# Taking a state-space scan's first half sequence inside an earlier stage, with its sum in SBUF

## The chip, the core and the metric

The kernel runs on one core of a Trainium2 chip. The time is device microseconds of one execution. The core has a matrix engine (PE, with a separate queue for loading weights, PEld), a vector engine (DVE), an activation engine (ACT), a general engine (POOL) and a queue that issues most of the transfers (SP). Each engine works off its own list of instructions in a fixed order; an instruction that has to wait holds up those behind it in the same list. All data are float32.

## The reference

Eight layers follow each other; each is a residual sum and a layer norm over x of shape 4 x 1024 x 128 (batch, sequence, features). The ones that matter here are the last four:

```
# linear attention with 16 heads of 64: running sums over the sequence
S_cos += k_cos v^T ; S_sin += k_sin v^T ; z_cos += k_cos ; z_sin += k_sin
out_t = (q_cos S_cos + q_sin S_sin) / max(q_cos z_cos + q_sin z_sin, 1e-6)

# top-2 mixture of 8 experts, hidden width 256
h = silu(gate) * up ; y = sum over the two chosen experts of weight * (h @ w2)

# state-space layer: 256 channels e, 16 states n
x = rmsnorm(resid) ; skip = x @ skip_w.T ; xs = silu(conv4(x @ in_w.T))
delta = softplus(...) ; B = xs @ wb.T ; C = xs @ wc.T
h[e,n] = exp(delta[e] * A[e,n]) * h[e,n] + delta[e] * xs[e] * B[n]    # over t
y[e]  = sum over n of h[e,n] * C[n]
out = resid + ((y + xs * W_D) * silu(skip)) @ out_w.T

# top-p mixture of 8 experts, hidden width 512, all experts computed
y = sum over e of gate[e] * (relu(x @ W1[e] + b1[e]) @ W2[e] + b2[e])
```

The scan over t of each (e, n) is a first-order recurrence. The two norms between these layers tie a batch's next layer to the end of its last one, but batches are independent of each other.

## The kernel before

x is held in SBUF twice for each batch: xN (tokens on partitions) and xT (features on partitions, 128 x 1024). A tile framework records the program in Python; generators yield between pieces, so that pieces of several layers are interleaved. The framework orders each engine's list itself, by the order in which the pieces were recorded and by its own estimate of when an operand is there; only PE's list inside the linear attention is kept as recorded (manual_schedule in l2_attn).

**Linear attention (l2_attn, line 920).** 128 units: 4 batches x 4 quarters of 256 tokens x 8 pairs of heads. A loop over t records pieces of units t to t + 2: l2_project makes q and k two units ahead (PE pqk, ACT r_q and r_k, and two POOL multiplications qt, L1059), l2_keys and l2_scores one unit ahead (kN on ACT, a on DVE), l2_before and l2_within consume qt and a, and l2_sums adds the running state (st on DVE). PSUM tiles pa, kp and po are single; qt has 3 buffers, a has 2.

**Top-2 experts (l2_dispatch, l2_ffn, l2_combine).** When a batch leaves the linear attention, l2_dispatch routes it on DVE and scatters its rows to DRAM with 16 indirect transfers from POOL (xrows, one with each step). l2_ffn then works through 23 tiles of 128 rows for each batch: rows 8 steps ahead, weights (wx, 384 KB, 4 buffers) 4 ahead, transposed tile 2 ahead, hidden layer, and two steps later the output. A step is one next() on the generator; the attention's loop makes one in each unit. When a unit 8 steps ahead belongs to a batch that has not been scattered, the whole pipeline stands. l2_combine gathers the outputs of a half batch back with 8 indirect transfers from POOL (yg), scales them on ACT and norms; a batch is marked "done" after its second half.

**State-space layer (l3, line 1595).** 8 half sequences (4 batches x 2 halves of 512 tokens). l3_prepare makes dl (delta), ud (delta times xs), xs and the rows of B and C in DRAM; its first call, for the very first half, is recorded inside the attention's loop once batch 0 is done, one piece in each unit, with batch 0 to 2's xT as scratch (l3_early, L1694). l3_scan (L1819) then takes 16 states n for each half. For each it issues two broadcasting transfers from SP (bn, cn: 128 x 512 each), one POOL multiplication db = ud * bn (L1849), two ACT exponentials da into PSUM (L1853), two DVE scans (L1854), one POOL multiplication hc = db * cn (L1865) and the sum over n by PE, a matmul with the identity for each of two channel halves (pys, L127). From batch 1 on, two states are first added by an accumulating transfer from POOL's queue (L1870), which halves those matmuls. l3_sum, l3_gate and l3_finish end a half: skip gate, output projection, norm, router. While half i is scanned, half i + 1 is prepared, half i - 1 is ended, top-2 tiles of later batches go on (one step a state, two in the first half), and three or four steps of the last layer's experts run.

**Last experts (l3_experts, l3_ffn).** For a half that has been ended for more than 3 states, 8 experts: 4 matmuls ph of 512 columns, ACT relu hh, 16 matmuls py, and a DVE accumulation h_acc each.

Of the kernel before, what the change touches and what calls it, by code (L numbers as in the profile page):

```python
# [10 lines left out]
F32 = mybir.dt.float32  # L11
# [47 lines left out]
class Net:  # L59
# [860 lines left out]
    def l2_attn(self, load, dispatch, moe, first):  # L920
# [7 lines left out]
        with ExitStack() as ctx:  # L928
# [25 lines left out]
            side, begin = [], None  # L954
# [9 lines left out]
            for t in range(-2, n + 4):  # L964
# [329 lines left out]
    def l2_dispatch(self, b):  # L1294
# [86 lines left out]
        for c in range(NC):  # L1381
            for k in range(2):
# [15 lines left out]
                yield  # L1398
# [3 lines left out]
    def l2_ffn(self, wp):  # L1402
# [8 lines left out]
        n = len(units)  # L1411
        side = []
        for t in range(-8, n + 4):
            while t + 8 < n and "put" not in units[max(t + 8, 0)]["st"]:
                for g in side[:]:
                    if next(g, self) is self:
                        side.remove(g)
                yield
            if 0 <= t + 8 < n and units[t + 8]["j"] % 4 == 0:
                self.l2_load_rows(units[t + 8], units, t + 8, wp)  # L1420
            if 0 <= t + 4 < n:
                self.l2_weights(units[t + 4], wp)
            if 0 <= t + 2 < n:
                self.l2_load_tile(units[t + 2], units, t + 2, wp)
            if 0 <= t < n:
                self.l2_hidden(units[t], wp)
            if 0 <= t - 2 < n:
                u = units[t - 2]
                self.l2_expert_out(u, units, t - 2, wp)
                if u["j"] == NT2 - 1:  # L1430
                    side.append(self.l2_combine(u["st"], wp))
# [4 lines left out]
        for g in side:  # L1436
            yield from g
# [81 lines left out]
    def l2_combine(self, st, wp):  # L1519
# [18 lines left out]
        for h in range(2):  # L1538
# [21 lines left out]
            yield from self.norm_parts(wp, acc, b, 4 * h, 4, ps=self.bank("ff"), act=True, slow=True, rows=False)  # L1560
        st["done"] = True
# [33 lines left out]
    def l3(self, moe, fp):  # L1595
# [12 lines left out]
        end = iter(())  # L1608
        for i, u in enumerate(halves):
            nxt = iter(())  # L1610
            if i + 1 < len(halves):
                if halves[i + 1]["h"] == 0:
                    while "done" not in self.m2["st"][halves[i + 1]["b"]]:
                        next(moe)
                nxt = self.l3_prepare(halves[i + 1])
# [594 lines left out]
```

## Time and profile before

| what | value |
|---|---|
| median of 3 runs (lowest, highest) | 2288.26 us (2287.27, 2295.73) |
| the profiled execution | 2286.79 us, its span 2285.0 us |
| busy in the span: PE, DVE, ACT, POOL | 87%, 59%, 53%, 45% |
| layers 1 to 4 | 0 to 615 us |
| linear attention, with top-2 experts woven in from 951 us | 615 to 1335 us |
| state-space layer and last experts | 1335 to 2285 us |
| first half's scan (first db to last hc) | 1390 to 1476 us |
| second half's scan | 1476 to 1569 us |
| tail after the last scan: last experts only | 2150 to 2285 us |

A line of the windows view gives, for a stretch of the span, the busy time of each engine with the number of its instructions, then the granted PE clock, the busy share of the transfer engines and GB/s. A line of the groups view gives source line, engine, operation, out<-in, shapes, count, then busy us and mean ns of one, then the idle time of the engine just before these instructions and what ended it. A line of a tile's view gives min/median/max ns of one.

### The profile page before, as it was taken

What the parts mean: (1) busy time and instruction counts of PE and PEld (TensorE: products, weight loads), DVE (VectorE), ACT (ScalarE), POOL (GpSimd) and SP (SyncE); (2) the same over time, 40 slices, a digit from 0 to 9 for tenths busy, and PEclk for the clock granted to TensorE, in tenths of its full rate; (3) what the DMA queues carried; (4) which work ended last, traced back from release to release, by engine and by line L of the source; (5) the groups of instructions that cost most, each with busy time, mean ns of one, the idle gap of its engine ahead of it and who ended that gap; (6) DMA issues with size and microseconds to landing.
All of it is one profiled execution on the core that took longest, in us unless ns stands there. A gap on an engine that the chain in (4) does not pass through costs nothing.

```text
span 2285.0 us, 46402 instructions
## 1 busy us (share of the span) xinstructions
PE 1978.9 (87%) x17806; PEld 1383.3 (61%) x17806; DVE 1349.2 (59%) x3693; ACT 1210.5 (53%) x2623; POOL 1023.4 (45%) x812
## 2 busy tenths in 40 slices
PE   6667979879999999999989876679899999999998
PEld 3455655444477777787767664246565656565666
DVE  6457843433355565565555555696777688776521
ACT  6543443332244444444455456576768786767443
POOL 5100230000023234224233418998889889879400
PEclk9667989979999999999999988799999999999999
DMA  3000110005000010031223147456786677776421
GB/s 107 0 14 24 30 39 1 19 10 174 1 3 2 3 35 15 17 87 49 65 80 85 37 126 221 135 175 200 216 216 178 174 189 192 193 187 167 119 61 51
DMA packets 138559, 211.10 MB, mean 92 GB/s; under 512 B 18598, under 2 KB 75937, under 8 KB 137953
## 3 DMA queue, kind: packets, MB, share of 16 engines
q1 hardware_dynamic: 126192, 173.87, 25.5%
q0 software_dynamic: 12144, 34.26, 7.1%
q8 instruction: 140, 2.29, 0.4%
q14 instruction: 83, 0.67, 0.1%
HBM read 160.29 MB, written 23.16 MB: 80 GB/s over the span
## 4 chain that ended last, share of the span: by engine, by line
PE 43%; DVE 12%; ACT 11%; issue 3%; DMA 2%; POOL 1%; SPq 0%; ACTq 0%; DVEq 0%; POOLq 0%
PE py L127 7%; PE ph L127 7%; PE po L1126 5%; PE pqk L127 5%; PE pa_m L127 5%; DVE db L1854 4%; PE pys L127 3%; PE kp_mo L127 3%; PE pv L127 2%; PE pr L1196 2%; ACT hh L1980 1%; ACT da L1853 1%; PE pt L131 1%; PE kp_mo L131 1%; ACT xN L174 1%
## 5 line engine op out<-in xcount | busy, mean ns | idle before, releaser
L1059 POOL TENSOR_TENSOR qt<-r_q,sb_c_turn 128x256 f32<-128x256 f32 (+1 forms) x256 | 164.0, 660 | 447.9 <-ACT r_q L1051 442.2
L1865 POOL TENSOR_TENSOR hc<-db,cn 128x1024 f32<-128x1024 f32 x128 | 314.7, 2493 | 57.1 <-PE pys L127 25.6
L127 PEld LDWEIGHTS py<-wh,hh 128*128 128x128 f32 x2048 | 249.8, 192 | 79.9 <-issue 44.8
L1849 POOL TENSOR_TENSOR db<-ud,bn 128x1024 f32<-128x1024 f32 x112 | 286.3, 2633 | 12.4 <-issue 9.9
L127 PE MATMUL ph<-xT,wh 128*128 128x512 f32 x512 | 256.3, 618 | 21.2 <-DVE h_acc L1996 5.8
L127 PE MATMUL py<-wh,hh 128*128 128x128 f32 x2048 | 258.2, 276 | 12.7 <-ACT hh L1980 6.6
L1980 ACT ACTIVATE hh<-ph,sb_cols 128x512 f32<-128x512 f32 x256 | 170.6, 680 | 131.1 <-PE ph L127 104.5
L1117 DVE TENSOR_TENSOR a<-pa_m,sb_c_near 128x256 f32<-128x256 f32 x256 | 96.6, 419 | 203.4 <-PE pa_m L127 203.4
L1074 ACT ACTIVATE kN<-kp_mo,sb_c_trig 128x128 f32<-128x128 f32 x448 | 129.8, 371 | 132.0 <-PE kp_mo L131 122.2
L1853 ACT ACTIVATE da<-dl,aneg 128x512 f32<-128x512 f32 x224 | 153.6, 689 | 74.4 <-DVE db L1854 73.3
L127 PE MATMUL pys<-hc,sb_c_ident 128*128 128x512 f32 x324 | 158.5, 619 | 22.7 <-POOL hc L1865 19.4
L1854 DVE TENSOR_TENSOR_SCAN db<-da,carry,db 128x512 f32<-128x512 f32 x128 | 156.9, 1265 | 11.7 <-ACT da L1853 8.8
L1854 DVE TENSOR_TENSOR_SCAN db<-da,db 128x512 f32<-128x512 f32 x128 | 149.3, 1205 | 10.4 <-POOL db L1849 6.0
L127 PEld LDWEIGHTS ph<-xT,wh 128*128 128x128 f32 x512 | 89.6, 196 | 104.7 <-issue 53.5
L1996 DVE SCALAR_TENSOR_TENSOR h_acc<-py,gt,h_acc 128x128 f32<-128x128 f32 x256 | 71.9, 342 | 125.8 <-PE py L127 125.8
L127 PE MATMUL pqk<-xT,wE 128*128 128x256 f32 x512 | 136.7, 390 | 8.3 <-ACT coT L1193 4.2
L127 PEld LDWEIGHTS pys<-hc,sb_c_ident 128*128 128x128 f32 x324 | 60.5, 199 | 86.7 <-issue 58.7
L729 POOL DMA_INDIRECT orows<-o,ix x20 | 18.9, 944 | 186.0 <-DVE o L727 160.4
L127 PEld LDWEIGHTS pqk<-xT,wE 128*128 128x128 f32 x512 | 88.5, 193 | 21.9 <-DVE cv L1036 8.1
L131 PE MATMUL pt<-sb_c_ident,xN 128*128 128x128 f32 x224 | 54.2, 345 | 51.0 <-ACT xN L174 31.8
L1193 ACT COPY coT<-pt 128x512 f32<-128x512 f32 x64 | 37.5, 586 | 114.9 <-PE pt L131 114.9
L127 PE MATMUL po<-ht,wD 128*128 128x512 f32 x192 | 93.7, 595 | 0.0
(456 smaller groups left out, 4344.1 us busy)
## 6 DMA issues: line engine op xcount, KB each, us to landing
wx<-in_wF SPq DMA_DIRECT2D x92, 384.0 KB, 3.4
bn<-rows SPq DMA_DIRECT2D x128, 256.0 KB, 5.0
cn<-rows SPq DMA_DIRECT2D x128, 256.0 KB, 4.2
wh<-in_wH SPq DMA_DIRECT2D x64, 512.0 KB, 3.8
hc<-hc POOLq DMA_DIRECT2D x47, 512.0 KB, 6.6
xrows<-zero SPq DMA_DIRECT2D x4, 1472.0 KB, 12.3
xg<-xrows SPq DMA_DIRECT2D x20, 256.0 KB, 3.0
yrows<-ys SPq DMA_DIRECT2D x20, 256.0 KB, 3.3
```

Of the source, the lines that this page charges most:

```text
L127: return self.nc.tensor.matmul(out=out, lhsT=lhsT, rhs=rhs, start=start, stop=stop)
L131: self.nc.tensor.transpose(out, in_, self.ident[0:n, 0:n])
L1059: nc.gpsimd.tensor_mul(u["qt"][:, m, a:], u["q"][:, a:], c2["turn"][:, m, o + a : o + 2 * P])
L1074: self.nc.scalar.activation(u["kN"][:, c, m, :], pk[:, c, :], AF.Copy, scale=trig[:, k, m : m + 1])
L1117: nc.vector.tensor_mul(u["a"][:, i, :, :], pa[i], self.c2["near"][:, None, :].to_broadcast([P, 2, P]),)
L1126: self.nc.tensor.matmul(out=u["po"][self.HALF[j], i, c, :], lhsT=lhsT, rhs=rhs, start=key not in u["begun"], stop=True, skip_group_check=True,
L1849: nc.gpsimd.tensor_mul(db, ud, bc[0])
L1853: nc.scalar.activation(da, dl[:, ec, :], AF.Exp, scale=aneg[:, j : j + 1])
L1854: nc.vector.tensor_tensor_scan(db[:, ec, :], da, db[:, ec, :], carry[:, ec, n : n + 1] if h else 0.0, ALU.mult, ALU.add,)
L1865: nc.gpsimd.tensor_mul(hc, db, bc[1])
L1980: nc.scalar.activation(ht, ph, AF.Relu, bias=self.col("h_b1", i=e * NK + k))
L1996: nc.vector.scalar_tensor_tensor(acc[:, c, :], py[:, c, :], gt[:, c, e : e + 1], acc[:, c, :], ALU.mult, ALU.add,)
```

## The change

Four parts.

1. The early preparation starts when batch 0's first half has been combined ("half"), not when both have. It is followed by a new generator l3_first, which takes the first half's 16 states inside the attention's loop. The recorded steps are spread evenly over the units that are left (left, 10 + 2 * 16 steps). Its working set differs from l3_scan's: bn, cn and db have 2 buffers; da goes to SBUF, one buffer for each channel half (the first is the weight tile wgru of the first layer); db is multiplied on DVE for odd n and on POOL for even n; and the sum over n is kept in SBUF in batch 0's xT (acc): n = 0 writes it, and each further state is added by an accumulating transfer from POOL's queue, each of which has to wait for the one before. The matmuls pys of this half are gone.
2. l2_ffn goes by the age of its tiles: each tile in flight passes stages at ages 0 (rows), 1 (weights), 3 (transposed tile), 5 (hidden), 7 (output), so tiles in flight go on when the next batch has not been scattered. The combining generators get two steps for each.
3. Batch 0's 16 scatters are recorded two to a step (no yield after the first of a pair for b = 0).
4. l3 no longer scans the first half: a prologue ends it while the second half is prepared, with one top-2 step and two scatter steps for each piece; then 7 halves are scanned, with two top-2 steps a state for the first two of them (halves 1 and 2). l3_gate moves from the scan into the end for halves where the scan hasn't made it.

The pool of the dispatch's tiles (md) is opened earlier. Cut to its core:

```diff
-                    if "done" in self.m2["st"][0]:
-
+                    if "half" in self.m2["st"][0]:
                         if begin is None:
-                            begin = self.l3_prepare(self.l3_early(first))
-                        next(begin, None)
+                            scan = ctx.enter_context(tc.tile_pool(name="scan", bufs=2))
+                            u = self.l3_early(first, scan)
+                            begin = chain(self.l3_prepare(u), self.l3_first(u, scan))
+                        for k in range(1 if "dl" not in u else max(1, -(-left // max(1, n - t)))):
+                            next(begin, None)
+                            left -= 1
...
-                yield
+                if k or b:
+                    yield
...
+        side, live, k = [], [], 0
+        stages = (
+            (0, lambda i: units[i]["j"] % 4 == 0 and self.l2_load_rows(units[i], units, i, wp)),
+            (1, lambda i: self.l2_weights(units[i], wp)),
+            (3, lambda i: self.l2_load_tile(units[i], units, i, wp)),
+            (5, lambda i: self.l2_hidden(units[i], wp)),
+            (7, lambda i: self.l2_expert_out(units[i], units, i, wp)),
+        )
+        while k < len(units) or live or side:
+            if k < len(units) and "put" in units[k]["st"]:
+                live.append([k, 0])
+                k += 1
+            for at, f in stages:
+                for i, age in live:
+                    if age == at:
+                        f(i)
+            for v in live:
+                v[1] += 1
+            if live and live[0][1] > 7:
+                i = live.pop(0)[0]
+                if units[i]["j"] == NT2 - 1:
+                    side.append(self.l2_combine(units[i]["st"], wp))
...
+            st["half"] = h
...
+        def ending(u):
+            for ec in range(2):
+                if len(u.get("gate", ())) == ec:
+                    self.l3_gate(u, ec)
+            yield from self.l3_sum(u)
+            yield from self.l3_finish(u)
+        end = ending(halves[0])
+        for f in following(0):
+            next(end, None)
+            next(moe, None)
+            for k in range(2):
+                next(self.m2["rest"], None)
+        for i, u in enumerate(halves[1:], 1):
+            nxt = following(i)
...
+                for k in range(2 if i < 3 else 1):
+                    next(moe, None)
...
+            if name == "ud":
+                return scan.tile(shape, F32, name=name, bufs=1)
...
+        u["acc"] = two(self.xT[0])
+        u["carry"] = pool.tile([P, 2, NST], F32, name="carry0")
+        u["wide"] = wide
...
+    def l3_first(self, u, pool):
+        nc, aneg = self.nc, self.c3["aneg"]
+        dl, ud, rows, acc, carry = (u[k] for k in ("dl", "ud", "rows", "acc", "carry"))
+        for n in range(NST):
+            bc = []
+            for i, nm in enumerate(("bn", "cn")):
+                t = pool.tile([P, 1, 512], F32, name=nm)
+                r = i * NST + n
+                nc.sync.dma_start(
+                    out=t[:, 0, :], in_=rows[r : r + 1, :].to_broadcast([P, 512])
+                )
+                bc.append(t.to_broadcast([P, 2, 512]))
+            db = pool.tile([P, 2, 512], F32, name="db")
+            (nc.vector if n % 2 else nc.gpsimd).tensor_mul(db, ud, bc[0])
+            yield
+            for ec in range(2):
+                j = ec * NST + n
+                da = pool.tile([P, 512], F32, name="da", bufs=1) if ec else u["wide"]
+                nc.scalar.activation(da, dl[:, ec, :], AF.Exp, scale=aneg[:, j : j + 1])
+                nc.vector.tensor_tensor_scan(
+                    db[:, ec, :], da, db[:, ec, :], 0.0, ALU.mult, ALU.add
+                )
+            nc.scalar.copy(carry[:, :, n : n + 1], db[:, :, 511:512])
+            hc = db if n else acc
+            nc.gpsimd.tensor_mul(hc, db, bc[1])
+            if n:
+                nc.gpsimd.dma_start(out=acc, in_=db, accum_op=ALU.add)
+            yield
+        u.update(py=[acc[:, ec, :] for ec in range(2)], sums=[])
```

More of the change, by code (lines that the diff above doesn't have):

```diff
@@ L953, in l2_attn @@
             n = len(units)
-            side, begin = [], None
+            side, begin, left = [], None, 10 + 2 * NST
             def early(moe):
@@ L1410, in l2_ffn @@
         ]
[L1411 to L1431, printed above, removed]
+        side, live, k = [], [], 0
[20 more added lines that the diff above has]
+                    side.append(self.l2_combine(units[i]["st"], wp))
             for g in side * 2:
@@ L1435, in l2_ffn @@
             yield
-        for g in side:
-            yield from g
     def l2_load_rows(self, u, units, i, wp):
@@ L1607, in l3, with following @@
         work = self.l3_experts(fp)
[L1608 to L1615, printed above, removed]
+        def following(i):
+            if i + 1 == len(halves):
+                return iter(())
+            if halves[i + 1]["h"] == 0:
+                while "done" not in self.m2["st"][halves[i + 1]["b"]]:
+                    next(moe)
+            return self.l3_prepare(halves[i + 1])
+        def ending(u):
[12 more added lines that the diff above has]
+            nxt = following(i)
             u["final"] = i + 1 == len(halves)
@@ L1622, in l3 @@
                     next(nxt, None)
-                for k in range(1):
-                    next(self.m2["rest"], None)
-                next(moe, None)
-                if i == 0:
-                    for k in range(1):
-                        next(moe, None)
+                next(self.m2["rest"], None)
+                for k in range(2 if i < 3 else 1):
+                    next(moe, None)
                 for k in range(4 if n % 8 == 7 else 3):
@@ L1634, in l3 @@
                 pass
-            end = chain(self.l3_sum(u), self.l3_finish(u))
+            end = ending(u)
         for f in end:
@@ L1692, in l3_at, with l3_early @@
         return pool.tile(shape, F32, name=name, tag=tag)
-    def l3_early(self, pool):
-        half = lambda b, i: self.xT[b][:, i * 512 : (i + 1) * 512]
+    def l3_early(self, pool, scan):
+        half = lambda i: self.xT[0][:, i * 512 : (i + 1) * 512]
+        two = lambda x: x.rearrange("p (e t) -> p e t", e=2)
+        wide = self.wgru.rearrange("p a b -> p (a b)")
         k = [0]
@@ L1702, in at @@
                 return pool.tile(shape, F32, name=name)
-            if name in ("dl", "ud"):
-                return self.xT[1 if name == "dl" else 2].rearrange("p (e t) -> p e t", e=2)
+            if name == "dl":
+                return two(self.xT[1])
+            if name == "ud":
+                return scan.tile(shape, F32, name=name, bufs=1)
             if name == "sq3":
-                return half(2, 0).rearrange("p (k d) -> p k d", d=D)
+                return half(0).rearrange("p (k d) -> p k d", d=D)
@@ L1707, in at @@
             if name == "db1":
-                return half(2, 1)[0:ND]
+                return wide[0:ND]
             if name == "xc":
                 k[0] += 1
-                return half(0, k[0] % 2)
-            return half(0, name == "sp_w")[:, None, :]
+                return half(k[0] % 2)
+            return half(name == "sp_w")[:, None, :]
         u = dict(b=0, h=0, at=at, ff=self.bank("pj"))
+        u["acc"] = two(self.xT[0])
+        u["carry"] = pool.tile([P, 2, NST], F32, name="carry0")
@@ L2177, in program @@
             w2 = ExitStack()
+            md = w2.enter_context(tc.tile_pool(name="moed", bufs=1, side="right"))
             n.l2_attn_load(w2.enter_context(tc.tile_pool(name="w2", bufs=1, side="right")))
@@ L2187, in program @@
         with w2:
-            md = w2.enter_context(tc.tile_pool(name="moed", bufs=1, side="right"))
             n.l2_attn(load, n.l2_dispatch, moe, first)
```

## The prediction

> **What bounds the kernel now.** I read the page first (shares and the 40 slices), then the windows by stage, the groups, the tile's view of gru_z and the transfers.
>
> ```profile
> PE 1978.9 (87%) x17806; PEld 1383.3 (61%) x17806; DVE 1349.2 (59%) x3693; ACT 1210.5 (53%) x2623; POOL 1023.4 (45%) x812
> PE   6667979879999999999989876679899999999998
> DVE  6457843433355565565555555696777688776521
> POOL 5100230000023234224233418998889889879400
> PEclk9667989979999999999999988799999999999999
> ```
>
> PE is the busiest engine, but not in every stage. The windows show it: us of the stretch, then busy time of PE, PEld, DVE, ACT, POOL.
>
> ```profile
> 960.00:1170.00 210.00, 198.72 (x3357) 166.66 (x3356) 126.59 (x470) 100.61 (x301) 64.78 (x99) 0.99 0.24 66
> 1170.00:1215.00 45.00, 34.27 (x497) 27.70 (x497) 22.31 (x92) 31.18 (x91) 20.81 (x27) 0.89 0.29 80
> 1335.00:1566.00 231.00, 163.88 (x741) 108.17 (x740) 161.16 (x326) 139.20 (x304) 186.97 (x104) 0.87 0.60 180
> 1566.00:2150.00 584.00, 533.16 (x2642) 346.31 (x2640) 437.92 (x844) 426.78 (x767) 510.32 (x263) 0.99 0.70 188
> 2150.00:2285.00 135.00, 120.87 (x678) 86.64 (x676) 33.05 (x118) 53.14 (x84) 0.00 (x0) 0.97 0.20 58
> ```
>
> In the linear attention (960 to 1170) PE is busy 95% of the time and POOL 31%. After it (1335 to 1566) PE falls to 71% while POOL, with the first two halves' multiplications, is at 81%: this is the hole that the change aims at. Later PE (91%) and POOL (87%) are both near full. The prices of the moved work:
>
> ```profile
> L1865 POOL TENSOR_TENSOR hc<-db,cn 128x1024 f32<-128x1024 f32 x128 | 314.7, 2493 | 57.1 <-PE pys L127 25.6
> L1849 POOL TENSOR_TENSOR db<-xT,bn 128x1024 f32<-128x1024 f32 x16 | 37.6, 2372 | 0.1
> L1854 DVE TENSOR_TENSOR_SCAN db<-da,db 128x512 f32<-128x512 f32 x128 | 149.3, 1205 | 10.4 <-POOL db L1849 6.0
> L235 DVE TENSOR_TENSOR_SCAN gru_h<-gru_a,gru_z 128x512 f32<-128x512 f32 x8 | 12.9, 1612 | 3.6 <-POOL gru_z L233 3.6
> ```
>
> Two lines of tiles' views (ns: min/median/max, then first to last start in us; the second within 1060 to 1160):
>
> ```profile
> L233 POOL TENSOR_TENSOR gru_z<-gru_z,gru_g x16: 1252/1749/2159, 12.0 to 57.7; 128x512 f32<-128x512 f32 x16
> L1051 ACT ACTIVATE r_q<-pqk,sb_cols x18: 473/482/511, 1064.1 to 1159.2; 128x256 f32<-128x256 f32 x18
> ```
>
> One line of the transfers (KB, us to landing) and one of PE's waits in 1160 to 1215 (us, times, longest):
>
> ```profile
> hc<-hc POOLq DMA_DIRECT2D x47, 512.0 KB, 6.6
> ...
> PE kp_mo L131 <- ACT ys L1510: 8.0, 4, 2.9
> ```
>
> To see: the scan takes 1.205 us with da in PSUM, but 1.61 us in the first layer, where both operands lie in SBUF and POOL multiplies beside it; POOL's 128x512 multiplication there took between 1.25 and 2.16 us, median 1.75. An accumulating transfer of 512 KB lands 6.6 us after its issue (median; shortest 4.5).
>
> **The change part by part.** The sum is made against the profiled execution, 2286.8 us; the median of the runs, 2288.3, is 1.5 us above it. 0.5% (11.4 us) is about what a measurement of this kernel can tell from no change.
>
> *Where the moved scan lands.* By the recorded order, combine of batch 0 now begins in unit 82 (before 102), half 0 is there in unit 88, the preparation ends in unit 99 (before 125), and the states are recorded one in two units, to 129. The lists of the engines say otherwise: in the built order POOL's 16 states stand between the qt of units 102 and 115, and DVE's scans between the a of units 101 and 114: 13 units, because the framework pulls ahead what it thinks ready. A unit there takes 5.88 us (34 r_q in 960 to 1160), so 76 us of attention carry the whole scan.
>
> *POOL in these 13 units.* 8 db and 16 hc: 24 x 2.36 = 57; 13 pairs of qt (0.728 each): 19; 15 issues of accumulating transfers (1.04): 16; 4 scatters: 4. Sum 96 us in 76. To this comes: (a) the scans' da is now in SBUF, as in the first layer. By gru_z's median over its minimum, 0.5 us for a multiplication of 512 columns, counted 0.5 to 1.0 for 1024: 12 to 24, taken 15. (b) Each accumulating transfer waits on POOL for the one before. Between neighbours in the list lie only 1.4 to 4.8 us of other POOL work in 9 of 14 cases; with 4.5 to 6.6 us to landing the waits add up to 12 to 31 us, taken 21. db has two buffers, so the product two states on waits for the same landing; I count that in the upper end. (c) hc waits for its scans: 57.1 us of idle over 128 = 0.45 each, 16 x 0.45 = 7. Together 139 us.
>
> *DVE in the same units.* Attention and tiles 3.15 us a unit (80.3 us in 1000 to 1150) = 41; batch 2's routing, some 45 small operations of 0.2, 10; 32 scans x 1.62 = 52; 8 products of 1024 columns, 2 x 0.684 (the nearest row, yg + yg, 128x512) = 11; the end of the preparation 3: 117 us. It is inside POOL's 139, but both lists run against PE's in a fixed order, so DVE is no way out. ACT has 32 exponentials x 0.69 + 16 copies x 0.19 = 25 us more on 48% busy, about 62 in 139: hidden. SP issues 32 broadcasts more; the transfer engines are at 24% here, so they are covered, but cn of state n + 2 stands in SP's list until hc of n is done, with a wx behind it; wx has 4 buffers, which cover a delay of about two units.
>
> *What it does to PE.* po of a unit needs its qt, which is made two units ahead; 8 us of lead are used up first. Loss in the attention: 139 - 76 - 8 = **+55**. Lower end: POOL's own work alone, 96 - 76 - 8 = +12. Upper end: 43 (gru_z's maximum, 0.9 for 512 columns, twice that for 24) and 31 for the waits, 7 for (c): 177 - 84 = +93. I take the middle because (a) and (b) are each taken at their typical row.
>
> A rule of the Trainium skill speaks against the change here: SBUF — State Buffer, Who interferes with whom, says that a DVE instruction with two SBUF inputs and a GpSimd one that reads SBUF exclude each other for the whole instruction. The gru rows agree in kind (1.61 against 1.205). Taken at full, 39 + 11 us of such DVE work would add to POOL's 96, 146 - 84 = +62, and the time would be 2311 instead of mine.
>
> *The second combine.* combine of batch 1 moves from after the attention into its last units (122 on). The same work cost before: 6 units in 1160 to 1215 instead of 9.4, 20 us, of which 8.0 are PE behind ACT's ys, which stands behind the scaling of gathered rows. Half of it falls past the last unit: **+10** (0 to +20). Batch 0's combine moves from 102 to 82 and costs the same there: 0.
>
> *Tiles by age.* 46 tiles instead of 43 are done in the attention: 3 x 1.9 us (8 rows 1.13, 4 rows 0.61, transpose 0.15) go from one side to the other: 0. Batch 0's scatters end in unit 52 instead of 60, each pair 2.5 us on a POOL that was idle 70%: 0.
>
> *After the attention.* Before: 55 us to the first db, 86 for half 0, 93 for half 1: 1335 to 1569, 234 us. After: a prologue to the first db of half 1, then its scan. The prologue must prepare half 1 (from 1346 to 1445, 99 us, beside a scan; 11 units, 65 us, in the attention), end half 0, run 14 tiles and pass the 8 gathers and 16 scatters (24 x 1.28 = 31 us of POOL): taken 80, between 60 and 99. The scan 93, plus 5 for gathers that move into it: 178 us, so -56. That holds the 27.5 us of PE that go (32 pys of 4 rows at 1.72 for two). Then 6 halves as before: POOL 87%, PE 91%, neither relieved in them. The tail doesn't shrink: in the built order some 317 last-expert matmuls stand behind the last half's pys against 296, because the experts, though begun sooner, go behind the denser tiles: 21 x 0.35 (7.0 us for an expert's 20) = +8 rounded. Together **-48** (-68 to -29).
>
> **Sum:** 2286.8 + 55 + 10 - 48 = 2303.8, **2304 us**, 0.7% slower.
>
> **The rivals.**
> *The attention covers the scan* (faster, the other side). For it: POOL idle 69% and DVE 40% between 960 and 1170. Against it: the 13 units. At the lower end: 2286.8 + 12 + 10 - 48 = 2261. It decides from the point where the 13 units take under 111 us (loss under 27 instead of 55).
> *Even.* A loss of 27 to 49: at 38, 2287.
> *The accumulating transfers set the pace.* Two buffers of db in a ring of product (2.4), scans (2.4), hc (2.4), issue (1.0) and landing (6.6), stretched by other POOL work: at a loss of 85, 2286.8 + 85 + 10 - 48 = 2334. For it: the 6.6 us. Against it: that median was taken at 70% busy transfer engines, here 24%.
> *The scan isn't taken inside the attention*: excluded by the built order, where the last hc stands 14 units before the end.
>
> **How the numbers follow.** Forecast (loss 49 to 75, 2298 to 2324) 0.38; deep 0.20; even 0.16; covered 0.26. Slower by over 0.5%: forecast and deep, 0.58; within: 0.16; faster: 0.26. The range 2255 to 2342 leaves about 0.1 on either side: the covered case with the prologue at 70 instead of 80, and the deep case up to a loss of 93.
>
> **What will show it.** In the profile after: units 102 to 115 at 9 to 11 us each instead of 5.9, with POOL near 90% busy and PE near 60% there; the new hc at over 2.6 us mean and its scans at 1.5 us or more; the end of the attention 55 to 70 us later than 1335; the first db of half 1 some 80 us after it; no pys for half 0; a tail of 135 to 145 us. Wrong if the units in the stretch stay under 8 us (then faster), or if the later halves fall under 90 us each with the tiles done sooner, which I have at nothing.

## The result and the profile after

The changed kernel takes 2358.8 us (median of 4 runs, 2354.1 to 2363.1) against 2290.1 us for the kernel before, run beside it on the same chip: a ratio of 1.030, 95% interval 1.028 to 1.032. It is slower, as forecast, but by 69 us and not by the 17 of the sum, and outside the range that was given. The profiled execution has a span of 2352.3 us, 67 us over the 2285.0 us of the profile before, and it is in the trace of this execution that the 67 us are looked for.

The page of the changed kernel: busy times, three of the 40-slice rows, two rows of the transfers.

```profile
PE 1989.4 (85%) x17742; PEld 1404.7 (60%) x17742; DVE 1380.2 (59%) x3707; ACT 1206.0 (51%) x2619; POOL 1025.7 (44%) x819
...
PE   6667978979999999997876697697869899899998
...
POOL 5100220000123252136255543689749978898500
PEclk9657989979999999998978797899979999999999
...
hc<-hc POOLq DMA_DIRECT2D x47, 512.0 KB, 6.6
xT<-db POOLq DMA_DIRECT2D x15, 512.0 KB, 5.9
```

The work is what it was: each engine's total is within 3% of before. What has changed is where PE idles. The attention's row of nines now breaks off at the 19th slice, five slices in a row stand at 6 to 8, and the granted clock falls to 7 or 8 in four of them. The 15 accumulating transfers on xT (the row `xT<-db`) are new.

The start of each unit's r_q on ACT, read from both traces, gives the ledger by stretch (us):

| from | to | before | after | difference |
|---|---|---|---|---|
| r_q of unit 59 | 73 | 66.7 | 84.7 | +18.0 |
| 73 | 102 | 172.9 | 195.3 | +22.4 |
| 102 | 115 | 101.6 | 168.0 | +66.4 |
| 115 | 127 | 77.1 | 74.2 | -2.9 |
| 127 | end | 962.2 | 925.9 | -36.3 |

In the kernel before, units from 102 on also hold the combine of batch 0 and units from 114 on its preparation, which the changed kernel does in units 82 to 99. So the first two rows are not all loss, and the third hides some: at the usual 5.88 us the 13 units would take 76 us, and their loss is 92.

The windows of the changed kernel, in columns as before (PE, PEld, DVE, ACT, POOL busy, then clock, share of the transfer engines, GB/s): the scan in the attention, then four stretches after it.

```profile
1181.00:1343.00 162.00, 110.76 (x1326) 93.26 (x1327) 115.55 (x243) 62.88 (x175) 96.20 (x73) 0.77 0.54 132
1435.00:1508.00 73.00, 47.21 (x296) 38.38 (x296) 45.29 (x160) 48.11 (x107) 25.37 (x25) 0.83 0.46 138
1508.00:1602.00 94.00, 80.38 (x396) 54.69 (x397) 68.64 (x104) 58.97 (x120) 83.86 (x42) 0.95 0.70 211
1602.00:1690.00 88.00, 72.13 (x406) 53.71 (x406) 59.06 (x108) 54.90 (x123) 77.86 (x43) 0.94 0.79 220
1690.00:1757.00 67.00, 44.32 (x169) 25.28 (x168) 38.67 (x104) 47.24 (x94) 25.69 (x22) 0.77 0.32 89
```

The first line is the key. POOL is busy 96.2 us in 162, 59%: the prediction had reckoned its work at 96 us and its occupancy at 90%. DVE is busy 115.6 us, and the prediction had reckoned 117. Both sums of work were right; the time that holds them wasn't. The last line is a hole after the attention that the kernel before doesn't have: there the stretches from one half's first scan to the next take 86 to 115 us, here half 2's takes 155.

What PE waited for in the scan's stretch (us in total, times, longest):

```profile
PE kp_mo L127 <- DVE st L1104: 23.7, 8, 5.3
PE pa_m L127 <- DVE a L1120: 13.6, 5, 5.2
PE pa_m L127 <- DVE mh L1497: 9.7, 5, 4.4
PE kp_mo L131 <- ACT ys L1513: 3.5, 2, 3.1
```

PE waits for three DVE instructions of the attention and of the tiles, 47 us of 52, and never for POOL's qt. These instructions take 0.28 to 0.41 us each; they are late because they stand in DVE's list behind scans and products. And that list stands still too: DVE waits 7.9 us there for landings of the accumulating transfers, POOL's multiplications 30.7 us for the carry copy that follows the scans, ACT's exponentials 27.6 us for the scans that still read their da.

The groups of the scan in the same stretch (busy time, mean ns of one, idle time before them and what ended it):

```profile
L1770 POOL TENSOR_TENSOR db<-db,cn 128x1024 f32<-128x1024 f32 x15 | 35.3, 2352 | 30.7 <-ACT carry L1768 30.7
L1765 DVE TENSOR_TENSOR_SCAN db<-sb_wA,db 128x512 f32<-128x512 f32 x16 | 27.4, 1712 | 3.9 <-POOL db L1759 3.9
L1765 DVE TENSOR_TENSOR_SCAN db<-da,db 128x512 f32<-128x512 f32 x16 | 21.9, 1368 | 0.0
L1759 DVE TENSOR_TENSOR db<-ud,bn 128x1024 f32<-128x1024 f32 x8 | 12.4, 1548 | 14.4 <-DMA xT<-db 7.9 <-issue 5.5 <-POOL qt L1062 1.0
```

POOL's multiplications by cn take 2.35 us, what the prediction had for them without contention; its 8 products by bn take 2.49 and its qt of 256 columns 0.85 (0.73 in the kernel before), some 5 us more in all. The scans' medians are 1.22 and 1.20 us; only a few are long, and those pull the mean to 1.54.

*The second part of the loss is slower matmuls.* PE was busy 110.8 us with 1326 matmuls. In the run without the scan (below, e1) the same kind of units took 138.45 us for 2336 matmuls at a clock of 0.99, 59.3 ns each; 1326 of them would be 78.6 us. So PE's own matmuls are 32 us longer, at a granted clock of 0.77, and 52 us are waits: together 84 of the 162 us, which leaves 78, about the 76 of 13 usual units. The ratio of the two mean clocks, 0.99 to 0.77, would make 101 us of the 78.6, so it covers 22 of the 32; the other 10 stay open.

### The profile page after: what moved, and what is told of

Its sections match the earlier page's. It is cut to its first block, busy times and chain, and to the rows that moved or that the text cites. A ratio compares the mean times of both kernels' runs of the same rounds, so it can differ in the third digit from the quotient of the medians.

```text
span 2352.3 us, 46187 instructions
## 1 busy us (share of the span) xinstructions
PE 1989.4 (85%) x17742; PEld 1404.7 (60%) x17742; DVE 1380.2 (59%) x3707; ACT 1206.0 (51%) x2619; POOL 1025.7 (44%) x819
## 5 line engine op out<-in xcount | busy, mean ns | idle before, releaser
L1062 POOL TENSOR_TENSOR qt<-r_q,sb_c_turn 128x256 f32<-128x256 f32 (+1 forms) x256 | 169.5, 684 | 418.5 <-ACT r_q L1054 414.9
L1907 POOL TENSOR_TENSOR db<-ud,bn 128x1024 f32<-128x1024 f32 x112 | 295.5, 2680 | 37.2 <-DVE ud L1871 21.0
L1923 POOL TENSOR_TENSOR hc<-db,cn 128x1024 f32<-128x1024 f32 x112 | 287.8, 2603 | 54.8 <-PE pys L127 27.4
L127 PEld LDWEIGHTS py<-wh,hh 128*128 128x128 f32 x2048 | 254.8, 194 | 79.2 <-issue 47.8
L127 PE MATMUL pqk<-xT,wE 128*128 128x256 f32 x512 | 141.6, 401 | 11.5 <-DVE cv L1039 7.8
L127 PE MATMUL pys<-hc,sb_c_ident 128*128 128x512 f32 x260 | 122.9, 598 | 4.2 <-DMA hc<-hc 4.2
L1912 DVE TENSOR_TENSOR_SCAN db<-da,db 128x512 f32<-128x512 f32 x96 | 112.4, 1206 | 6.3 <-ACT da L1911 5.8
L127 PE MATMUL pa_m<-r_q,r_k 64*64 64x128 f32 x2048 | 91.2, 292 | 9.7 <-DVE mh L1497 9.7
L127 PEld LDWEIGHTS pa_m<-r_q,r_k 64*64 64x64 f32 x2048 | 58.1, 138 | 55.1 <-issue 39.9
```

What stands on the lines that cost most here:

```text
L127: return self.nc.tensor.matmul(out=out, lhsT=lhsT, rhs=rhs, start=start, stop=stop)
L1062: nc.gpsimd.tensor_mul(u["qt"][:, m, a:], u["q"][:, a:], c2["turn"][:, m, o + a : o + 2 * P])
L1907: nc.gpsimd.tensor_mul(db, ud, bc[0])
L1912: nc.vector.tensor_tensor_scan(db[:, ec, :], da, db[:, ec, :], carry[:, ec, n : n + 1] if h else 0.0, ALU.mult, ALU.add,)
L1923: nc.gpsimd.tensor_mul(hc, db, bc[1])
```

## The experiments

The chips differ: beside some of the runs the kernel before takes 2287 to 2290 us, beside others 2333 to 2340. Ratios are to the kernel before on the same chip. The changed kernel itself was measured on both kinds: 1.030 on the one, 1.034 (1.030 to 1.038) on the other. Differences below 0.004 between the two kinds are not read. The traces of e1, e2, e3, e5, e6, e7, e8, e17, e18 and c_after are from the slower kind, where 5.88 us a unit become about 6.0.

**The scan left out, and the changed kernel again.** e1 removes the states' loop and keeps everything else.

```
-        for n in range(NST):
-            bc = []
...
-            yield
+        nc.vector.memset(carry, 0.0)
+        for n in range(2 * NST):
+            yield
```

> The 16 states of the first half's scan are left out of the attention (no broadcasts, products, scans, multiplications, accumulating transfers; the carry is set to zero, and the half's sum is whatever its tile holds), so this times the rest of the change alone. Theory 1 (the scan itself is the loss in the attention): its 13 units, 168 us in the changed kernel, fall back to about 80, and the time to 2358.8 - 88 = about 2270 us. Rival (the loss is in the moved tiles, the earlier combine and the earlier preparation): the attention still ends over 60 us later than before, and the time stays above 2320 us.

> The changed kernel itself, unedited, beside the three edits that follow: every theory expects the ratio found before, 1.030 (1.028 to 1.032).

Measured: e1 2319.8 us, ratio 0.994 (0.991 to 0.998); c_after 1.034. Theory 1 holds: the scan in the attention is worth 0.036 to 0.040 of the time, 82 to 92 us, and units 102 to 115 fall from 168.8 us to 85.8. But 0.994 says something else as well. This kernel doesn't compute the first half's scan at all, neither in the attention nor after it, and it is only 0.6% faster than the kernel before, although the scan and its stretch took 86 us there. So the rest of the change must lose much of what it wins: the prediction had it at 38 us to the good (+10 and -48), and it is 13. e10 looks for where. The stretch of e1 and its largest wait:

```profile
1216.00:1362.00 146.00, 138.45 (x2336) 118.16 (x2337) 84.64 (x315) 70.63 (x216) 46.64 (x65) 0.99 0.30 84
```

```profile
PE kp_mo L127 <- DVE st L1104: 5.1, 3, 2.2
```

24 units in 146 us, PE busy 95%, clock 0.99, and the wait for st down from 23.7 us in 13 units to 5.1 in 24.

**Without the accumulating transfers.**

```
             nc.gpsimd.tensor_mul(hc, db, bc[1])
-            if n:
-                nc.gpsimd.dma_start(out=acc, in_=db, accum_op=ALU.add)
             yield
```

> The 15 accumulating transfers of the first half's sum are left out (the half's sum then holds state 0 alone); products, scans and multiplications stay. Theory 2 (the transfers set the pace: a ring of product 2.4, scans 2.4, multiplication 2.4, issue 1.0, landing 5.9 us for every two states' buffers): the 13 units shrink by 31 us or more, the time to 2300 to 2328 us. Theory 3 (the states are too dense in engine lists of fixed order; the landing was waited for only 7.9 us on DVE and 3.4 on POOL in the changed kernel's profile): only these waits and 13 us of issues go, the time stays at 2335 us or above.

Measured: 1.0228 (1.0209 to 1.0246), 0.011 under c_after on the same kind of chip, some 26 us; 2385 us where the expectation, moved to this chip's scale (2333 for 2288), has 2345 to 2374 for theory 2 and 2381 or above for theory 3. Theory 3 holds. The trace adds a reason: with the transfers gone the framework packs the 16 states into 10 units (102 to 112, 134 us) instead of 13, and PE's wait for st rises to 44.0 us. The transfers cost something, but they don't set the pace: without them the states stand closer and PE waits longer for DVE.

**The states spread.**

```
-            (nc.vector if n % 2 else nc.gpsimd).tensor_mul(db, ud, bc[0])
+            i = (nc.vector if n % 2 else nc.gpsimd).tensor_mul(db, ud, bc[0]).ins
+            self.tc.add_manual_dep(i, self.beat.name, SYNC, reason="spread out")
             yield
```

> Each state's first product waits for the r_q activation that was recorded last before it, so that the states keep the recorded pace of one in two units (units 102 to the end of the attention instead of 102 to 115). Same work. Theory 3 (density): with 11.8 us of attention for a state, its DVE and POOL work fits beside the units; the scan's loss falls from 92 us to between 30 and 50, the time to 2297 to 2317 us. Rival (each state costs PE the same wherever it stands: about 5.7 us, 92 over 16): within 10 us of 2358.8.

Measured: 1.0222 (1.0205 to 1.0239), about 27 us under c_after; neither theory's number (as ratios, 1.004 to 1.013 and 1.027 to 1.035). The trace shows both halves of it. In the attention the spread does what theory 3 said: from unit 102 to 127 it takes 209 us against 248 in c_after and 165 in e1, so the loss falls from 83 us to 44. But the last states fall past the last unit (the last two multiplications by cn start 38 and 42 us after its r_q), and from there to the scan of half 1 it is 120 us instead of 97. A state costs the attention about 3.4 us here (44 over 13) and about 5.2 when packed (83 over 16).

**One link at a time.** e6 takes POOL's multiplication out of the chain, e7 DVE's scans.

```
-            hc = db if n else acc
-            nc.gpsimd.tensor_mul(hc, db, bc[1])
+            if n == 0:
+                nc.gpsimd.tensor_mul(acc, db, bc[1])
```

> In the scan inside the attention the multiplication by cn, 2.36 us on POOL, is left out for states 1 to 15 (the accumulating transfers then add the scans' own results); scans, products and transfers stay. The scan as a whole was worth 0.036 of the time before (1.030 with it, 0.994 without). Theory P (POOL's work, and DVE instructions that wait for POOL's to end, set the pace): at least half comes back, the ratio falls to 1.012 or below. Theory D (DVE's list, 128 us busy in 168, sets the pace, and PE waits for what stands in it behind scans): at most a quarter, 1.021 or above. Theory C (the chain product, scans, copy, multiplication, each link alike): a third, 1.015 to 1.020.

```
-                nc.vector.tensor_tensor_scan(
-                    db[:, ec, :], da, db[:, ec, :], 0.0, ALU.mult, ALU.add
-                )
```

> In the scan inside the attention DVE's 32 scans are left out (the products go unscanned into the multiplication; the carry copies the product's last column); exponentials, products, multiplications and transfers stay. Theory D: at least 0.022 of the 0.036 comes back, the ratio falls to 1.008 or below. Theory P: at most 0.011, 1.019 or above. Theory C: about a third to a half, 1.012 to 1.018.

Measured: e6 1.0221 (1.0187 to 1.0255), e7 1.0195 (1.0162 to 1.0229), where the changed kernel on the same chip had 1.0338. Theory D has e6 and misses e7 by far, theory P has e7 and misses e6 by far. Theory C is 0.002 under both, less than the 0.004 by which the changed kernel itself stands higher on this chip than the expectations took it; by the share of the 0.040 that comes back (0.012 and 0.014, three tenths and a third) it is the nearest. Leaving out 35 us of POOL's work, or 49 us of DVE's, brings back about the same 27 to 33 us of the whole.

The traces don't bear out that each link counts alike. From unit 102 to 127 c_after takes 248 us and e1 165; e7 takes 217 and e6 238, so without DVE's scans 31 of the 83 us come back in the attention, without POOL's multiplications only 10 (and 17 in e2, without the transfers). The rest of e6's gain lies behind the attention (934 us from r_q of unit 127 to the end, against 945 in c_after), where e7 loses (958). Nor is the pace of the states the same: in e2 and e6 the framework packs them into 10 units. What the runs do show is that no one quantity of work is the bound: with no scan at all on DVE 52 us of the loss stay, and in e7 PE still waits 19.8 us for a and 18.6 for st, while DVE's products wait for POOL's qt (16.9 us) and for landings (4.8). DVE's list weighs most; that the rest comes from product, scans, copy, multiplication and transfer each waiting for the one before, in lists of fixed order on four engines, is argued from these waits.

**All products on POOL.** More work for the engine that the prediction held to be the bound, less for the one that PE waits for.

```
-            (nc.vector if n % 2 else nc.gpsimd).tensor_mul(db, ud, bc[0])
+            nc.gpsimd.tensor_mul(db, ud, bc[0])
```

> In the scan inside the attention all 16 products by bn are made by POOL, where odd ones were DVE's: DVE loses 8 x 1.5 = 12 us of work and the waits for landings and for POOL that stood ahead of these products in its list (21 us in the last run of the changed kernel); POOL gets 8 x 2.4 = 19 us more. Theory D2 (PE waits for DVE's attention instructions, 55 us of its 60 us of waits there, because they stand behind scans and products that wait): the 13 units shrink by 20 to 35 us, the ratio falls from 1.030 to 1.034 to 1.016 to 1.025. Theory P (POOL sets the pace, as the prediction had it): the ratio rises to 1.036 or above.

Measured: 1.0203 (1.0186 to 1.0220), 2333.2 us, 22 us faster than the changed kernel's 1.030 on this kind of chip. Theory D2's number; theory P falls. The same 162 us of the two kernels, for e11 here, for the changed kernel in the first window above:

```profile
1185.00:1347.00 162.00, 114.19 (x1554) 94.81 (x1550) 120.59 (x270) 70.64 (x198) 124.64 (x88) 0.85 0.58 142
```

POOL is busy 124.6 us instead of 96.2, and PE gets through 1554 matmuls instead of 1326, in hardly more busy time because the clock is 0.85 instead of 0.77. Units 102 to 115 take 139.5 us instead of 168.0, and r_q of unit 127 comes 19 us sooner. PE's waits are still for st and a (46 us), none for qt, but the same 46 us now lie in 15 units instead of 13.

**The hole after the attention.** e3 gives the tiles the pace of before in the later halves; e9 lets the last experts begin one half later.

```
-                for k in range(2 if i < 3 else 1):
+                for k in range(2 if i < 2 else 1):
                     next(moe, None)
```

> After the attention the experts' tiles are stepped twice per state in the loop's first half alone, once from the next on, as in the kernel before. Theory 4 (batch 3's tiles, done sooner, put its combine beside the preparation of the fourth half, and that is the hole from 1694 to 1757 us): the hole falls from 63 to some 20 us, the time by 25 to 40, to 2319 to 2334 us. Rival (the tiles and the combine cost the same wherever they stand): within 10 us of 2358.8.

```
-                for k in range(4 if n % 8 == 7 else 3):
+                for k in range(0 if i == 1 else 4 if n % 8 == 7 else 3):
                     next(work)
```

> The last experts' generator isn't stepped in the loop's first half (half 1), so that their matmuls begin one half later. In the changed kernel the end of half 1 (its po) stands in PE's list behind 123 of these matmuls (46 in the kernel before) and ran at 1688 us, 47 us after its input was ready; the preparation of half 3 came behind it, and POOL waited 21 us for it in the hole from 1694 to 1757 us. Theory 5 (that place in PE's list is the cause of the hole): the scans of half 3 start within 110 us of those of half 2 instead of 155, the tail grows by some 10 us, and the time falls by 20 to 40 us: a ratio of 1.014 to 1.024 against 1.030 to 1.034. Rival (the hole moves elsewhere, since the same work remains): 1.028 or above.

Measured: e3 1.0293 (1.026 to 1.0326) beside c_after's 1.0338 on the slower chips, e9 1.0319 (1.0301 to 1.0336) beside 1.0299. Neither gains anything that stands outside the intervals; theories 4 and 5 both fall. In e3 the hole stays where it was (154 us from half 2's first scan to half 3's); e1, without the scan, has it too (156 us). In e9 it moves: half 2 takes 120.5 us instead of 155.2, but half 1 114.6 instead of 93.7, and the stretch from the last half's first scan to the end grows from 222 to 236 us. Why moving it is worth nothing shows in the windows from the attention's end to the kernel's end; of the kernel before, of the changed kernel, and of e9:

```profile
1335.00:2285.00 950.00, 817.91 (x4057) 541.13 (x4055) 632.13 (x1287) 619.12 (x1152) 697.30 (x367) 0.95 0.60 167
```

```profile
1435.00:2352.00 917.00, 787.67 (x3978) 529.76 (x3978) 589.99 (x1231) 583.84 (x1073) 615.77 (x327) 0.94 0.57 159
```

```profile
1435.00:2364.00 929.00, 793.35 (x4034) 536.51 (x4034) 593.00 (x1240) 581.27 (x1074) 615.06 (x327) 0.94 0.56 157
```

PE is busy 86%, 86% and 85% of the three. POOL's work fell by 82 us, DVE's by 42; PE's fell by 30, and the stretch got shorter by 33. The first half's scan was a hole for PE, but PE's remaining work was in it: tiles, routing and preparation that now need a place of their own, beside later halves where PE is about 90% busy. That the stretch follows PE's work is argued from these three windows; which of the waits inside the hole would have to go first stays open.

**The parts without the scan.** e10 is the kernel before with the experts' tiles by age (the changed kernel's `l2_ffn`) and batch 0's scatters two to a step, preparation from unit 114; e8 is the same with the preparation at its earlier place, where it overwrites inputs that the attention has still to read.

```
-                yield
+                if k or b:
+                    yield
...
-                    if "done" in self.m2["st"][0]:
+                    if "done" in self.m2["st"][0] and t > 113:
```

> The kernel before with two parts of the change alone: the experts' tiles go by their age, and batch 0's scatters two to a step; the scan stays after the attention. The prediction had these parts at nothing: 0.997 to 1.003. Rival (a combine and a preparation that fall into units without a tile cost more than among tiles: units 85 to 99 took 103 us in the run without the scan, against 72 in the kernel before): 1.005 to 1.012.

> The kernel before with the experts' tiles by age and batch 0's scatters two to a step, and the first half's preparation begun in unit 114 as in the kernel before; its scan stays after the attention. (The earlier run of these two parts also began the preparation at unit 88, where it overwrote inputs of the attention that were still to be read, which put further waits into it.) The prediction has these parts at nothing: 0.997 to 1.003. Rival (a combine in units without a tile isn't covered by tiles): 1.004 to 1.010.

Measured: e8 1.0125 (1.0093 to 1.0157), e10 1.0182 (1.0165 to 1.0199), 42 us. Both are over the rival's range, and far from the prediction's nothing. Of e10's 50 us over the profile before, the attention has 33 (r_q of unit 127 at 1355.6 us against 1322.8) and the time after it 17, though three tiles and a combine have left that stretch. Three further edits split it: the scatters alone, the tiles' order alone (the same two hunks, one at a time), and both with the tiles held after batch 1's tile 19.

```
-                    early(moe)
+                    if t <= 119:
+                        early(moe)
```

> The kernel before with batch 0's scatters two to a step alone; the tiles go as before, the preparation begins in unit 114 as before. The two parts together were 1.018. If the earlier tiles (some 8 units) as such are the cost: 1.008 or above. If the order of the tiles' work by age is: within 1.000 +- 0.003 here.

> The kernel before with the experts' tiles by their age alone; scatters one to a step, preparation from unit 114. If the order by age is the cost (tiles of one batch go on without the pause of the kernel before, and the combine follows among units without tiles): 1.012 or above. If the earlier tiles are: 1.003 or below. If they add: 1.006 to 1.011.

> Both parts, preparation from unit 114, but the tiles stop in the attention after tile 19 of batch 1 (unit 119), so that its last 3 tiles and its combine are done after the attention, as in the kernel before. Theory 6 (these lay in the stretch after the attention beside idle PE, where they cost little, and inside the attention they cost their time): the attention ends 15 to 25 us sooner than with both parts, and the ratio falls from 1.018 to 1.004 to 1.010. Rival (the loss lies in batch 0's tiles and combine): 1.014 or above.

Measured: scatters alone 1.0014 (1.0000 to 1.0028), nothing; the order by age alone 1.0180 (1.0146 to 1.0213), all of it; with batch 1's last tiles and its combine held back 1.0081 (1.0049 to 1.0114), so 0.010, some 23 us, is theirs. Theory 6 has the ratio, but only in part the place. It expected the attention to end 15 to 25 us sooner than in e10: r_q of unit 127 comes 9 us sooner (1346.2 us against 1355.6; 13 us if counted from unit 59). The other 17 us lie behind it: from r_q of unit 127 to the end e16 takes 961.8 us, as before (962.2), against 979.0 in e10, although e16 has more to do there. So with these tiles in the attention the attention is longer and the stretch behind it is longer too; why the latter is open.

The other 0.008 stays in the attention: 438 us from unit 59 to 127 in e16 against 418 before. Batch 0's tiles now run without their pause, so units 59 to 73 take 84.7 us instead of 66.7, and its combine falls into units 85 to 99 that hold no tile. In the kernel before, units without a tile are the cheap ones (87 to 93 took 4.6 us each); in e10 the same units take 6.6, and PE idles there. The windows from 1060 to 1150 us, of the kernel before and of e10:

```profile
1060.00:1150.00 90.00, 85.98 (x1498) 71.73 (x1498) 47.99 (x167) 41.27 (x119) 29.61 (x48) 1.00 0.21 57
```

```profile
1060.00:1150.00 90.00, 71.49 (x1301) 56.36 (x1300) 40.57 (x140) 39.78 (x111) 47.76 (x62) 0.91 0.12 33
```

Units 85 to 99 take 10 us more in e10 than before, and units 102 to 115, which the combine has left, 10 less; so what the earlier tiles cost in units 59 to 73 isn't won back later. No run moves batch 0's combine alone.

**Do the edits add?**

```
-                        for k in range(1 if "dl" not in u else max(1, -(-left // max(1, n - t)))):
+                        for k in range(1 if "dl" not in self.c3["first"] else 1 + t % 2):
...
-            (nc.vector if n % 2 else nc.gpsimd).tensor_mul(db, ud, bc[0])
+            i = nc.gpsimd.tensor_mul(db, ud, bc[0]).ins
+            self.tc.add_manual_dep(i, self.beat.name, SYNC, reason="spread out")
...
-                for k in range(4 if n % 8 == 7 else 3):
+                for k in range(0 if i == 1 else 4 if n % 8 == 7 else 3):
```

> Three edits together: states at one in about 1.3 units, each held to the r_q activation recorded last; all products by bn on POOL; the last experts from the second half of the loop on. If the gains add (spread 0.010, products 0.010, experts 0.012): 1.000 to 1.008. If the spread and the products cure the same wait: 1.010 to 1.016.

> The changed kernel with the tiles' order of the kernel before (not by age) and all products by bn on POOL. In the built order three of the 16 states then stand in the attention (from unit 122 on), the rest after it, beside the preparation of half 1; the first half's sum is still taken in SBUF. If the measured parts add: 1.030 to 1.034, less 0.018 for the tiles' order, less 0.010 to 0.013 for the products, is 0.999 to 1.006, and less what 13 states cost in the attention, if they hide beside the preparation: 0.98 to 0.99. If POOL (73 us for 13 states with their issues) and DVE become the bound of the stretch after the attention: 1.00 to 1.02.

> The changed kernel with all products by bn on POOL, and with the tiles stopped in the attention after tile 19 of batch 1, so that its last tiles and its combine come after the attention. If the two edits add (0.010 each, as measured apart): 1.008 to 1.013. If the combine costs as much beside the prologue as in the attention: 1.018 to 1.022.

e17 takes `l2_ffn` of the kernel before into the changed one, with e11's edit; e18 is e11 with e16's. Measured: e13 1.0222 (1.0203 to 1.0241), no better than the products on POOL alone (1.0203); e17 1.0334 (1.0300 to 1.0369); e18 1.0298 (1.0262 to 1.0334). None of the sums came true. In e18 the held tiles, worth 0.010 on the kernel before, make the time longer than with the products on POOL alone: from r_q of unit 127 to the end it is 984 us, where e11 has 923 (944 on e18's chip). In e13 the attention ends 10 us sooner than in e11, and the stretch after it is 15 us longer. In e17, where most states are done after the attention beside the preparation, the way from unit 127 to half 1's first scan is 201 us, where it was 156 in the kernel before (159 on this chip's scale). So the prediction's own habit, to price parts one by one and add them, fails for the edits as well: whatever leaves one stretch has to be done in another, and PE is nearly full in all but a few. No version that computes the whole result beats the kernel before.

## Why the prediction was wrong

*The place.* Right: the states stand between units 102 and 115, and the stretch begins and ends there.

*The ledger.* The sum had +17 and the result is +69. e1 parts the 52 us between: the scan is worth 82 to 92 us instead of 55, and the rest of the change wins 13 us instead of 38. The direction was right, but by a path that the runs refute.

*The scan in the attention, +55.* This is the first step that failed; e1 puts it at 82 to 92 us. The prediction took POOL for the pace ("po of a unit needs its qt"): 96 us of work plus 43 of contention and waits. The work was right in sum (96.2 us), and DVE's too (115.6 against 117). But PE never waited for qt. It waited 47 us for st, a and mh on DVE, and when POOL was given 19 us more and DVE 12 less (e11), the time fell by 22 us. The sentence "it is inside POOL's 139 ... so DVE is no way out" had seen the list that mattered and left it out of the sum. By the terms: (a), 15 us of longer multiplications on POOL, was some 5, in qt and the products by bn; (b), 21 us of POOL waiting for landings, was 3, with 4 more that the profile gives no cause for, and 8 on DVE; (c), 7 us of hc waiting for scans, was 30.7. "ACT ... hidden" failed too, since its exponentials, with one da buffer for each of the two, waited 27.6 us for the scans and held up what stood behind them. And a term was missing altogether: PE's matmuls at a lower clock, 32 us longer, of which the clock's mean covers 22. The scans' 1.62 us was a mean that hid two kinds, in the first layer as here: medians of 1.22 and 1.27 us there, single scans up to 2.28.

*The second combine +10, tiles by age 0.* This is the second step that failed: on the kernel before, the parts together cost 42 us (e10), of which the order by age is all and the scatters nothing, as predicted for these. "3 tiles ... go from one side to the other: 0" would need both sides to be equally full. They weren't: the prediction's own windows gave PE 71% after the attention and 95% in it. Batch 1's last tiles and combine cost 23 us by being moved in (e16): some 9 to 13 in the attention, near the +10, and the rest behind it, where the prediction had nothing. How much of the 42 is in the changed kernel, no run parts; e1 says only that all without the scan fell 25 us short. "Batch 0's combine moving from 102 to 82: 0" was priced at the same cost in both places, without asking whether the units at the new place hold a tile.

*After the attention, -48.* The sum came near (-36), but not its parts. From the last r_q to half 2's first scan it is 175.6 us instead of 251.2, 76 less, where the prediction had 56 less. Then "6 halves as before" failed: from half 2's first scan to half 7's it is 528.0 us against 487.2, 41 more: half 2 takes 155 us instead of 99, half 3 82 instead of 115, halves 4 and 5 together 18 more. The tail, +8, was right: 132 us against 125 from the last pys to the end; the last half before it took 9 us less.

*The rivals.* "The accumulating transfers set the pace" had the loss nearly right (85 us) and the mechanism wrong: without them only 26 us come back (e2). "The attention covers the scan" fell by a wide margin, 168 us for the 13 units where 111 was its limit.

*What should show it.* Units at 9 to 11 us: they took 12.9. POOL near 90%: 59%. PE near 60%: 68%, at a clock of 0.77. hc above 2.6 us: 2.35. Scans at 1.5 us or more: 1.54 in the mean, by a few long ones. The attention's end 55 to 70 us later: 104. No pys for half 0: so it is.

*The range* was wide only for the 13 units and the prologue. The parts that were put at nothing had no bounds.

## What to carry to other kernels

Reckon a stretch from the list that the bounding engine waits on, not from the engine with the most added work: here PE hung on three short DVE instructions, and long instructions put ahead of them in a list of fixed order cost more than their own length (62 us of scans and products on DVE, 82 to 92 us of time). Work that is moved "from one side to the other" costs the difference in how full the two sides are, and, as far as the three windows show it, work taken out of a hole shortens the whole only by what the bounding engine had to do there. A wait that makes the bounding engine idle is paid twice where the idling also lowers its clock.

## What the runs showed of the hardware that was not expected

*The granted TensorE clock is lower where PE has gaps.* 0.99 where PE is busy 95% (e1's 24 units); 0.85 at 70% (e11), 0.77 at 68% (the changed kernel), for units of the same kind. In the changed kernel the matmuls are 32 us longer, 22 of them by the ratio of the mean clocks; in e5 by the same reckoning 19, 17 of them by a clock of 0.88 (2348 matmuls in 158.0 us, against 139.2 at 59.3 ns). The Trainium skill (TensorE: Matmul & The Clock Gate, Part 1: The HAM clock gate) describes a clock that is passed in full only while the array stays busy, and at half when it has idled; the windows here agree in direction, with means in between.

*DVE can wait for the whole of a POOL multiplication.* One stretch of the changed kernel's timeline (start us, duration us):

```profile
1238.83 2.36 POOL L1759 TENSOR_TENSOR db<-ud,bn 128x1024 f32<-128x1024 f32 x1
1238.88 2.33 DVE L1370 CAST di<-chd 128x8 int32<-128x8 f32 x1
...
1241.14 2.40 POOL L1770 TENSOR_TENSOR db<-db,cn 128x1024 f32<-128x1024 f32 x1
...
1241.52 2.10 DVE L1372 TENSOR_TENSOR ch<-ch,rt_p 128x64 f32<-128x64 f32 x1
```

A cast of 8 columns takes 2.33 us (0.15 elsewhere), a multiplication of 64 columns 2.10 (0.21), and both end within 0.1 us of POOL's instruction. Between 1184 and 1352 us thirteen DVE instructions, six of them scans, took over 0.4 us longer than the shortest of their form, each beside one of POOL's, 18.7 us in all. The prediction had weighed the Trainium skill's rule (SBUF — State Buffer, Who interferes with whom) against the first layer's rows and charged contention to POOL. For scans and multiplications the rule is what is seen, and DVE pays most: 18.7 us, where POOL's qt and products by bn lost some 5. The casts and copies among the thirteen, four of them, have one input and aren't in the rule as the prediction tells it. At its full reach, every DVE instruction with two SBUF inputs, the prediction had 50 us; 26 of the 32 scans took less than 0.4 us over the shortest.

*A landing is hardly shorter where the transfer engines are less busy.* The accumulating transfers into xT land 5.9 us after their issue (median) at 54% busy transfer engines, against 6.6 later at about 70%.
